# Reordering the hand-over from a linear recurrent layer to attention: convolutions, logits and GELUs issued at other places

## The chip, the cores and the metric

The kernel runs on one core of a Trainium2 chip. A core has five engines that matter here: TensorE (PE: matrix products and transposes), VectorE (DVE), ScalarE (ACT: activations), GpSimd (POOL) and SyncE (SP, which here only issues DMAs). Each engine works through its own list of instructions in order and waits on semaphores for the others. The metric is the device time of one execution in microseconds (us); the median of several runs is compared.

## The reference, cut to what matters

One transformer-like block on x of shape (4, 1024, 256) in float32:

```python
x = x + lru(layernorm(x))     # linear recurrence over time, then an MLP with exact GELU and a layer norm
x = x + ffn(layernorm(x))     # the "first FFN"
x = x + attention(layernorm(x))   # 8 heads of 64, keys and values from a rank-64 latent
x = x + ffn(layernorm(x))     # the "last FFN", same weights
```

The FFN is the unusual part. For each token it forms two score vectors of 256 (`so` and `si`):

```python
xc = einsum('ngf,gf->ng', x.reshape(n, 64, 4), conv_w) + conv_b    # a grouped "convolution": 256 -> 64
xn = (xc - mean_over_tokens) * rsqrt(var_over_tokens + eps) * gamma + beta
score = softmax(gelu(xn) @ lin_w.T + lin_b)
top 32 of 256 scores are kept, all others are zero
out = (x @ W) * top32(score_so) + (x * top32(score_si)) @ W + bias
```

The mean and the variance go over all 4096 tokens. So no GELU of an FFN can start before the last token has passed through the layer before it and its convolution.

## The kernel before

**Tiles.** The 4096 tokens are 32 tiles of 128 tokens (128 partitions, 256 features). Four tiles are a block; there are 8 blocks (NBLK), two for each of the four batch rows. x stays on chip in float32 for the whole kernel, and every sublayer updates it in place.

**Order of the work.** The program is Python that issues instructions through generators. A generator (`head`, `tile`, `outputs`, `ahead`, `prepare`) yields at stage borders, and the loops in `tile_kernel` advance several of them by turns with `next`. A scheduler of the framework then orders the instructions of each engine by a simulated timeline; `with tc.issue_after(ins)` keeps what is issued inside it behind the named instruction. So the diff moves calls, and what it does to an engine's order has to be read from the built program.

**The LRU's end (lines 1105 to 1116).** `outputs` (L422) makes the LRU's output for a block: products into `po`, bias to `ot` (L438), a product into `pz` and GELU to `zt` (L446), a second product `pz2` (added to `ot` on VectorE, L455), transposes to `py` (L465), layer norm (statistics on VectorE, applied on ScalarE as `yn`, L474), and the update of x (L479, L480). For the last block, number 7, this is done in two halves of 256 tokens, and line 1110 fixes how their steps alternate. `f1.head(blk)` (L501) is the first FFN's start for a block: layer norm statistics of the updated x, normalised tiles `xn` (ScalarE, L145), transposes to `pt` (TensorE, L147), a copy `ft` (ScalarE, L524), which also goes to DRAM as `tt` through SP's queue (L527), the convolution `pc` (TensorE, L529), its bias to `xc` (ScalarE, L533), and statistics of `xc` (VectorE, L534). A head has two pairs of tiles, each with its own `xn`, `pt`, `ft`. Heads 0 to 4 are issued earlier; head 5 behind the last GELU of the LRU, head 6 behind the last `yn`, head 7 in two halves at the end.

**The first FFN's first eight tiles (lines 1126 to 1168).** `norm_scale` (L538) turns the statistics into `bs` and `bt`. `gelu(blk)` (L585, instruction at L587) applies GELU to one block of `xc` in place, on ScalarE. GELU and Exp are in different activation tables; `warm` (L151) issues one tiny activation so that the table is loaded at a chosen place. `tile(i)` (L589) does one tile: logits into `pl` (TensorE, L554 and L556), the largest 8 (VectorE, L674), `nm` (GpSimd, L613), exponentials `ex` and `e` (ScalarE, L615 and L618); then three more rounds of max and match_replace on VectorE (L674) and the difference `ex` (L628); then the output branch `pf` (TensorE, L567) scaled to `ob` (ScalarE, L650); then the input branch `xg` (ScalarE L657, times `ex` at L658), transposed to `px` (L682), copied to `vt` (ScalarE, L697), multiplied into `pf` (L699) and added to x (VectorE, L662). `ahead(blk)` (L571) computes the products `pfa` of later blocks (L567), copies them to `pfs` (ScalarE, L581) and stores them (L582). `pf` and `pfa` share two PSUM buffers, `px` has one, `pl` two (line 1129). Only blocks 0 and 1 are tiled here; the other 24 tiles are worked off inside attention, so the GELUs of blocks 2 to 7 are not read before that. `attn_weights` prepares the attention weights beside it, and `prepare`, `latents`, `values` and `queries` (keyed by the loop index in `places`, line 1148) start attention's first batch row: layer norm, `xn`, `pt`, `xnt`, latent product `pml` (L170), `kh` and `kl`. Attention proper begins with the first score product `sc` (L881).

**The rest.** Attention (`heads`, L856) runs with a list of side jobs placed by `merge` (L952), and the last FFN (from line 1198) runs 32 tiles like the eight above, with one GELU ahead and seven behind the exponentials of an early tile.

Of the kernel before, what the change touches and what calls it, by code (L numbers as in the profile page):

```python
# [26 lines left out]
TPB = T // P  # L27
# [123 lines left out]
def warm(nc, pool, func):  # L151

    t = pool.tile([P, 1], F32, tag="warm", name="warm")
    nc.gpsimd.memset(t, 0.0)
    nc.scalar.activation(t, t, func)
# [818 lines left out]
def run(*gens):  # L974
    for g in gens:
        for _ in g:
            pass
# [51 lines left out]
def tile_kernel(ctx: ExitStack, tc: tile.TileContext, x_in, w_lru, vecs_in, rows, w_ffn, lin_t, w_attn, w_down, out):  # L1029
# [34 lines left out]
    with ExitStack() as c1:  # L1064
        psum = Banks(c1.enter_context(tc.tile_pool(name="ps1", space=PSUM)), {"pu": 2, "po": 2, "py": 2, "pt": 2})

        brow = c1.enter_context(tc.tile_pool(name="brow", bufs=1)).tile([P, 2, D], F32, tag="brow", name="brow")
        lru = Lru(tc, c1, ident, vecs, brow, w_lru, psum)
        xb = [x[4 * k : 4 * k + 4] for k in range(NBLK)]
        xnt = [lru.head(xb[0])]  # L1070
        lru.tables(lambda: xnt.append(lru.head(xb[1])))
        with tc.issue_after(lru.xnt_first):
            for blk in range(2, 4):
                load_x(nc.scalar, blk)
        h = [[lru.states(xnt, c) for c in range(KD)]]
        lru.output_weights()
        with tc.issue_after(lru.evacuated[3]):
            nc.scalar.dma_start(brow.rearrange("p a b -> p (a b)"), rows[0, 2 * D : 4 * D].partition_broadcast(P))
        xnt += [lru.head(xb[k]) for k in (2, 3)]
        h.append([lru.states(xnt[2:4], c) for c in range(KD)])  # L1080
        for k in range(NBLK):
            last = k >= NBLK - 2
            if k == 0:
                with tc.issue_after(lru.evacuated[7]):
                    for blk in range(4, NBLK):
                        load_x(nc.scalar, blk)
                    ffn_weights(
                        nc, c1.enter_context(tc.tile_pool(name="rows", bufs=1)), cp, w, lint, lin_t, w_ffn, rows
                    )
            if k < NBLK - 1:  # L1090
                run(lru.outputs(k % CH, xb[k], xnt[k], h[k // CH], (0, 1), last))

            b = k // CH + 1
            if 2 <= b < B:
                if k % CH == 0:
                    h.append([])
                h[b].append(lru.states(xnt[b * CH : (b + 1) * CH], k % CH))
            if k + 4 < NBLK:
                xnt.append(lru.head(xb[k + 4]))
            if 2 <= k < NBLK - 2:  # L1100
                run(f1.head(k - 2, lru.sp, psum, "pt"))
        for blk in range(4, NBLK - 3):
            run(f1.head(blk, lru.sp, psum, "pt"))
        k = NBLK - 1
        ot, zt = lru.buffers()
        halves = [
            lru.outputs(k % CH, xb[k], xnt[k], h[k // CH], (i,), last, tag, [v[:, :, c : c + 256] for v in (ot, zt)])
            for i, tag, c in ((0, "pu", 0), (1, "po", 256))
        ]
        for i in (0, 0, 1, 0, 1, 0, 1, 0, 1, 1):  # L1110
            next(halves[i])
        with tc.issue_after(lru.last_gelu):
            run(f1.head(NBLK - 3, lru.sp, psum, "pt"))
        with tc.issue_after(lru.last_yn):
            run(f1.head(NBLK - 2, lru.sp, psum, "pt"))
        run(*(f1.head(NBLK - 1, lru.sp, psum, "pu", (i,), "lx", "zt") for i in range(2)))

    with ExitStack() as c2:
        sp = c2.enter_context(tc.tile_pool(name="at_s", bufs=2))
        wp = c2.enter_context(tc.tile_pool(name="at_w", bufs=1))  # L1120
        two = lambda shape, name: [wp.tile(shape, F32R, tag=f"{name}{i}", name=f"{name}{i}") for i in range(2)]
        wqk, wvo, wd = two([P, KD, HEADS * HD], "wqk"), two([P, PAIRS, D], "wvo"), two([P, KD, P], "wd")
        wfs = two([P, KD, D], "wf")
        nc.scalar.copy(wfs[0], w.wf)
        nc.gpsimd.tensor_tensor(wfs[1], w.wf, wfs[0].bitcast(F32), ALU.subtract)
        at = Attention(tc, x, ident, ident64, wqk, wvo, wd, sp, wp)
        with ExitStack() as c4:
            psum = Banks(
                c4.enter_context(tc.tile_pool(name="ps4", space=PSUM)), {"pl": 2, "px": 1, "pf": 2, "at": 3}
            )  # L1130
            fp = c4.enter_context(tc.tile_pool(name="f_t", bufs=4))
            weights = attn_weights(nc, fp, psum, "at", w_attn, w_down, wqk, wvo, wd, at, ident64)
            f1.norm_scale(sp)
            tts = [f1.load(blk, fp, f"tt{blk}") for blk in range(2)]
            f1.gelu(0)
            with tc.issue_after(f1.gelu(1)):
                for blk in range(2, NBLK):
                    g = f1.gelu(blk)
            with tc.issue_after(g):
                warm(nc, sp, AF.Exp)  # L1140
            tiles = [
                f1.tile(i, fp, psum, ("pl", "px", "pf"), fast=i == TPB - 1, tt=tts[i // 4]) for i in range(TPB)
            ]
            aheads = chain(*(f1.ahead(blk, fp, psum, "pf") for blk in range(2, NBLK)))
            first = at.prepare(0, 0, psum, "at")
            second = at.prepare(0, 1, psum, "at", ((0, 1), (2,), (3,)), False)
            queries = at.queries(0, 0, 0, psum, "at")
            places = {4: [first] * 2, 5: [first] * 2 + [at.values(0, 0, psum, "at")], 7: [queries] + [second] * 4}
            f1.keep = True
            next(tiles[0])  # L1150
            logits = f1.last_logits
            for i in range(TPB + 1):
                if i + 1 < TPB:
                    next(tiles[i + 1])
                if i < TPB:
                    next(tiles[i])
                    next(tiles[i])
                    with tc.issue_after(logits):
                        next(weights, None)
                if i:  # L1160
                    run(tiles[i - 1])
                for steps in places.get(i, []):
                    next(steps)
                for _ in range(2 if i else 0):
                    next(aheads, None)
            run(second)
            f1.keep, f1.last_topk = False, None
        psum = Banks(c2.enter_context(tc.tile_pool(name="ps2", space=PSUM)), {"sc": 2, "t": 2, "s": 2})
        at.hp = c2.enter_context(tc.tile_pool(name="at_h", bufs=1))
        fp = c2.enter_context(tc.tile_pool(name="f_s", bufs=2))  # L1170
        side = []
        for b in range(B):
            n = STEPS * b
            side += [
                (n + nb * 32 + 8 * g - 7, at.queries(b, nb, g, psum, "s"), 1)
                for nb in range(2)
                for g in range(PAIRS)
                if b or nb or g
            ]
            side.append((n + 33, at.output(b, 0, psum), 1.5))  # L1180
            side.append((n + STEPS - 1 if b == B - 1 else n + STEPS + 1.5, at.output(b, 1, psum, range(2 if b == B - 1 else 4)), 1 if b == B - 1 else 1.5))
            side.append((n + 40 if b == B - 1 else n + STEPS + 24, f2.head(2 * b, sp, psum, "s"), 2))
            last = b == B - 1
            side.append((n + STEPS if last else n + STEPS + 8, f2.head(2 * b + 1, sp, psum, "s", (0,) if last else (0, 1)), 1 if last else 2))
            if b < B - 1:
                side.append((n + 38, chain(at.prepare(b + 1, 0, psum, "s"), at.values(b + 1, 0, psum, "s")), 1.5))
                side.append((n + 56, chain(at.prepare(b + 1, 1, psum, "s"), at.values(b + 1, 1, psum, "s")), 1.5))
        side.append((1, at.values(0, 1, psum, "s"), 1))
        for i in range(TPB, NT):
            n = i - TPB  # L1190
            start = 1 + 6.75 * n if n < TPB else STEPS * (n // TPB) - STEPS + 48.25 + 8 * (n % TPB + 1)
            side.append((start, f1.tile(i, fp, psum, "sss", parts=wfs, fine=True), [1, 1, 1, 1, 1, 2, 1]))
        merge(chain(*(at.heads(b, psum) for b in range(B))), side)
        run(at.output(B - 1, 1, psum, range(2, 4)), f2.head(NBLK - 1, sp, psum, "s", (1,)))
# [107 lines left out]
```

## Time and profile before

| what | us |
|---|---|
| median of 3 runs (1536.07 to 1539.59) | 1538.0 |
| the profiled execution's own time | 1533.81 |
| span of its instructions | 1532.1 |
| busy: PE / DVE / ACT / POOL | 1297.4 / 1182.9 / 1014.5 / 681.6 |
| last convolution output `xc` of the first FFN starts (L533) | 291.55 |
| first GELU starts (L587) | 296.48 |
| first exponential starts (L615) | 303.94 |
| first score product of attention starts (L881) | 378.31 |
| first GELU of the last FFN starts (L587) | 1330.91 |

All times within the execution are from the span's start. The span is what the profile shows from first to last instruction; the execution's own time is 1.7 us longer, and both belong to one execution, which is 4.2 us shorter than the median of the runs. A line of a timeline names start, duration, engine, source line, operation, output and input with their shapes and a count, and in brackets how long the engine was idle before it and what released it. Consecutive instructions of one kind are merged.

### The profile page before, as it was taken

Reading aid. Unit: us, or ns where it says so; the run is one execution under the profiler, and the core shown is the slowest. Engines: PE = TensorE matmul, PEld = TensorE weight load, DVE = VectorE, ACT = ScalarE, POOL = GpSimd, SP = SyncE. Lnnn points to the kernel's source line nnn. Section 1 sums busy time; section 2 is a strip of 40 time slices with the busy share of each in tenths; the row PEclk is TensorE's granted clock in tenths of the full one; section 3 lists DMA queues with packets and bytes.
Section 4 is the critical chain, followed back from the end, with each engine's and each line's share of the span. In section 5 each row is a group of like instructions: output and inputs, shape, how many; then the busy total and the mean of one; then the engine's idle time right before and its main releaser. Section 6 shows DMA issues by size and latency. Waiting matters only on the chain. (4 is left out here: it accounts for less than half of the span.)

```text
span 1532.1 us, 28693 instructions
## 1 busy us (share of the span) xinstructions
PE 1297.4 (85%) x10136; PEld 960.2 (63%) x10136; DVE 1182.9 (77%) x3674; ACT 1014.5 (66%) x2145; POOL 681.6 (44%) x848
## 2 busy tenths in 40 slices
PE   4879998698898898898998889888999998657786
PEld 3635455365676766766776767677777776334554
DVE  8976665697878887878778687777676675499998
ACT  5353433664787777787777787877777776476664
POOL 2033333162545454544543554454443534157776
PEclk9999999698999999999999999999999999789888
DMA  3010000331454334344433345434444454000000
GB/s 117 32 41 15 21 21 14 135 101 44 76 91 90 70 70 80 67 80 77 85 76 60 65 85 81 66 60 85 78 75 88 83 95 83 1 11 24 25 25 28
DMA packets 288609, 96.51 MB, mean 63 GB/s; under 512 B 268233, under 2 KB 284626, under 8 KB 288466
## 3 DMA queue, kind: packets, MB, share of 16 engines
q1 hardware_dynamic: 283024, 88.50, 29.0%
q10 hardware_dynamic: 5442, 6.18, 1.2%
q8 instruction: 80, 1.31, 0.3%
q14 instruction: 63, 0.52, 0.1%
HBM read 16.01 MB, written 11.53 MB: 18 GB/s over the span
## 5 line engine op out<-in xcount | busy, mean ns | idle before, releaser
L893 POOL TENSOR_TENSOR pd<-pr,pd 128x1024 f16<-128x1024 f32 x128 | 273.5, 2142 | 256.5 <-ACT pd L892 198.6
L885 DVE TENSOR_REDUCE nm<-sc 128x1 f32<-128x1024 f32 x256 | 308.5, 1218 | 76.8 <-PE sc L881 75.3
L889 ACT ACTIVATE pr<-sc,nm 128x1024 f32<-128x1024 f32 x256 | 285.9, 1120 | 89.8 <-DVE nm L887 53.3
L881 PE MATMUL sc<-kh,qs 128*128 128x512 f32 x512 | 184.9, 439 | 27.1 <-ACT pr L889 19.5
L881 PE MATMUL sc<-kl,qs 128*128 128x512 f32 x512 | 162.4, 398 | 0.0
L674 DVE MATCH_REPLACE8 wk<-m,wk 128x256 f32<-128x256 f32 x384 | 158.3, 419 | 0.1
L905 ACT COPY p<-ptp 128x512 f32<-128x512 f32 x224 | 124.3, 590 | 46.3 <-PE ptp L900 38.2
L900 PE MATMUL ptp<-ident,pr 128*128 128x128 f32 x1024 | 140.2, 277 | 15.6 <-ACT pr L889 14.8
L674 DVE MAX8 m<-wk 128x8 f32<-128x256 f32 x384 | 153.0, 424 | 0.4
L925 PE MATMUL pmo<-p,la 128*64 128x128 f32 x2048 | 142.3, 287 | 5.6 <-ACT ft L524 2.9
L900 PEld LDWEIGHTS ptp<-ident,pr 128*128 128x128 f32 x1024 | 117.1, 141 | 38.0 <-ACT pr L889 24.9
L892 ACT CAST pd<-pr 128x1024 f16<-128x1024 f32 x128 | 133.3, 1055 | 5.9 <-DMA d<-pd 4.8
L925 PEld LDWEIGHTS pmo<-p,la 128*64 128x64 f32 x2048 | 121.5, 143 | 24.2 <-ACT ft L524 5.1
L881 PEld LDWEIGHTS sc<-kh,qs 128*128 128x128 f32 x512 | 85.6, 196 | 51.9 <-ACT pr L889 30.8
L881 PEld LDWEIGHTS sc<-kl,qs 128*128 128x128 f32 x512 | 97.1, 190 | 23.4 <-issue 1.4
L925 PE MATMUL pmo<-d,lb 128*64 128x128 f16 x3072 | 101.8, 221 | 7.6 <-DVE qs L853 2.5
L925 PEld LDWEIGHTS <-lb 128*64 128x64 f16 x3072 | 91.2, 111 | 25.4 <-issue 19.5
L628 POOL TENSOR_TENSOR ex<-ex,wk 128x512 f32<-128x512 f32 x61 | 77.6, 1273 | 50.8 <-DVE wk L674 41.7
L921 POOL COPY rows<-rs 128x128 f32<-128x128 f32 x128 | 36.2, 295 | 125.5 <-PE pmo L933 69.3
L936 DVE TENSOR_TENSOR on<-pmo,rb 128x128 f32<-128x128 f32 x128 | 36.5, 285 | 66.8 <-ACT rb L935 66.2
L699 PE MATMUL pf<-wf,vt 128*128 128x256 f32 x288 | 84.4, 438 | 3.6 <-ACT vt L697 3.6
L147 PE MATMUL pt<-ident,xn 128*128 128x128 f32 x256 | 48.2, 308 | 42.5 <-ACT xn L145 30.6
(306 smaller groups left out, 2789.0 us busy)
## 6 DMA issues: line engine op xcount, KB each, us to landing
tt<-ft SPq DMA_DIRECT2D x16, 256.0 KB
tt<-tt SPq DMA_DIRECT2D x8, 512.0 KB
out<-x SPq DMA_DIRECT2D x32, 128.0 KB
x<-in_x ACTq DMA_DIRECT2D x6, 512.0 KB
pf<-pfs SPq DMA_DIRECT2D x12, 256.0 KB
full<-pf SPq DMA_DIRECT2D x24, 128.0 KB
d<-pd SPq DMA_TRANSPOSE x128
wa<-in_w_attn SPq DMA_DIRECT2D x2, 640.0 KB
```

The costliest lines, as they stand in the source:

```text
L147: nc.tensor.transpose(pt[:, k, i * P : (i + 1) * P], xn[:, k * P : (k + 1) * P], ident)
L628: pool.tensor_tensor(ex, ex, wk, ALU.subtract)
L674: ins = make(*args).ins
L699: nc.tensor.matmul(dst, vt[:, k, :], w.wf[:, k, :], start=(k == 0 and bias is None), stop=(k == KD - 1))
L881: nc.tensor.matmul(sc[:, sl], qs[:, j, q * P : (q + 1) * P], kk[:, sl], start=(i == 0), stop=(i == 1))
L885: nc.vector.tensor_reduce(nm, sc, AX.X, ALU.max, negate=True)
L889: nc.scalar.activation(pr, sc, AF.Exp, bias=nm, accum_out=ssum[:, j : j + 1])
L892: nc.scalar.copy(pd[:, 0, :], pr)
L893: nc.gpsimd.tensor_tensor(pd[:, 1, :], pr, pd[:, 0, :], ALU.subtract)
L900: nc.tensor.transpose(pt[:, kk, :], pr[:, kc * P : (kc + 1) * P], self.ident)
L905: nc.scalar.copy(dst, pt)
L925: nc.tensor.matmul(po[j * HD : (j + 1) * HD, 0, :], v, pts[j][:, c, :], start=(n == 0), stop=(n == len(terms) - 1),)
```

## The change

Three edits in `tile_kernel`. First, head 5 of the first FFN is issued after three steps of block 7's halves, with no condition, and head 6 behind the LRU's last GELU; before, these were the last GELU and the last `yn`. Second, the third step of a tile (difference, `pf` and `ob`) is moved inside the `with` that puts it behind the first tile's logits. Third, the GELUs of blocks 2 to 7 are issued behind the exponentials of tile 7, and with them a second `warm(Exp)`; the first `warm(Exp)` comes behind the GELU of block 1.

```diff
-        for i in (0, 0, 1, 0, 1, 0, 1, 0, 1, 1):
+        for i in (0, 0, 1):
+            next(halves[i])
+        run(f1.head(NBLK - 3, lru.sp, psum, "pt"))
+        for i in (0, 1, 0, 1, 0, 1, 1):
             next(halves[i])
         with tc.issue_after(lru.last_gelu):
-            run(f1.head(NBLK - 3, lru.sp, psum, "pt"))
-        with tc.issue_after(lru.last_yn):
             run(f1.head(NBLK - 2, lru.sp, psum, "pt"))
         run(*(f1.head(NBLK - 1, lru.sp, psum, "pu", (i,), "lx", "zt") for i in range(2)))
...
             f1.gelu(0)
             with tc.issue_after(f1.gelu(1)):
-                for blk in range(2, NBLK):
-                    g = f1.gelu(blk)
-            with tc.issue_after(g):
                 warm(nc, sp, AF.Exp)
...
                 if i + 1 < TPB:
                     next(tiles[i + 1])
+                if i + 2 == TPB:
+
+                    with tc.issue_after(f1.last_exp):
+                        for blk in range(2, NBLK):
+                            g = f1.gelu(blk)
+                    with tc.issue_after(g):
+                        warm(nc, sp, AF.Exp)
                 if i < TPB:
                     next(tiles[i])
-                    next(tiles[i])
                     with tc.issue_after(logits):
+                        next(tiles[i])
                         next(weights, None)
```

## The prediction

> **What bounds the kernel now.** I read the page's table of 40 slices, then a table of busy time by stage, then ScalarE's timeline, then the chain of waits at the end. In the slices:
>
> ```profile
> PE   4879998698898898898998889888999998657786
> DVE  8976665697878887878778687777676675499998
> ACT  5353433664787777787777787877777776476664
> PEclk9999999698999999999999999999999999789888
> ```
>
> A slice is 38.3 us. Slice 8 (268 to 306 us) is where the LRU hands over to the first FFN: TensorE drops to 6 tenths, its clock to 6. The change acts only from 250 to 378 us; the 920 us of attention and the last FFN keep their instructions. By stage:
>
> ```profile
> core 0: us, PE busy (x) PEld busy (x) DVE busy (x) ACT busy (x) POOL busy (x), PEclk, DMA share, GB/s
> 250.00:272.00 22.00, 22.00 (x116) 17.69 (x114) 12.62 (x54) 7.63 (x16) 5.52 (x8) 1.00 0.04 12
> 272.00:292.10 20.10, 11.46 (x49) 5.15 (x50) 12.66 (x84) 12.48 (x24) 0.10 (x1) 0.64 0.22 76
> 296.50:305.10 8.60, 7.38 (x24) 5.09 (x25) 2.24 (x10) 8.57 (x17) 1.68 (x4) 0.72 0.82 311
> 305.10:359.00 53.90, 51.62 (x235) 37.08 (x235) 53.00 (x235) 32.73 (x92) 31.13 (x45) 0.94 0.28 98
> 359.00:378.30 19.30, 13.98 (x57) 10.22 (x55) 12.59 (x49) 7.79 (x17) 1.79 (x3) 0.78 0.04 14
> ```
>
> TensorE is full until 272 (22.00 of 22.00), then nothing is: a latency chain through all four engines, at a clock of 0.64. From 296.5 ScalarE is full (8.57 of 8.60) while VectorE does 2.24 us. From 305.1 to 359 VectorE is full (53.00 of 53.90): the top-32 of eight tiles. The last 19 us are again a chain. ScalarE's timeline in the two holes:
>
> ```profile
> 276.15 1.01 ACT L474 ACTIVATE yn<-py,ly_rs 128x256 f32<-128x256 f32 x2
> 278.28 1.02 ACT L474 ACTIVATE yn<-py,ly_rs 128x256 f32<-128x256 f32 x2 [1.12 <-DVE ly_rs L136]
> 279.19 1.09 ACT L145 ACTIVATE xn<-x,norm_f 128x256 f32<-128x256 f32 x2
> 284.44 1.09 ACT L145 ACTIVATE xn<-x,norm_f 128x256 f32<-128x256 f32 x2
> 291.55 0.47 ACT L533 ACTIVATE xc_f<-pc,vecs 128x256 f32<-128x256 f32 x1 [1.22 <-PE pc L529]
> 296.48 5.75 ACT L587 ACTIVATE xc_f<-xc_f,bt,bs 128x512 f32<-128x512 f32 x8 [2.98 <-DVE bt L548]
> 302.24 1.28 ACT L155 ACT_TABLE_LOAD   x1
> 303.94 0.47 ACT L615 ACTIVATE ex<-pl,nm 128x256 f32<-128x256 f32 x1
> ```
>
> Block 7's LayerNorm applies at 276.15 and 278.28; then head 6 (from 279.19) and head 7 (from 284.44) follow until the last convolution output at 291.55. All statistics wait for that, so GELU starts at 296.48; eight of them and a table load hold the first exponential until 303.94. The last FFN, in the chain that ended last, has the shape that the change gives the first:
>
> ```profile
> 1330.91 0.82 ACT xc_f L587
> 1331.78 2.09 PE pl L556 x2
> 1333.89 0.78 DVE m L674 x2
> 1334.97 0.56 ACT ex L615 x2
> ```
>
> From one GELU to the first exponential it takes 4.06 us; here it is 7.46 (303.94 - 296.48).
>
> **What the Trainium skill says.** "ScalarE: Activation LUTs", section "What ACT_TABLE_LOAD costs": a switch is 1283 ns of load plus some 1380 of drain. The trace agrees on the load (1.28), but the next ScalarE instruction is there 0.01 us later, so I take 1.3. "TensorE: Matmul & The Clock Gate", "What's actually happening": after an idle window of about 3.4 us the array runs at half speed, until as long a busy one. The trace agrees: after 4.33 us idle four transposes take 1.18 us (279.84), before it 0.60 (271.34). Same page, "Architectural detail: the array is 16× 32×32, not 1× 128×128": ScalarE and VectorE are strict FIFOs. So the order of the built program, which I compared on each engine, fixes who queues behind whom.
>
> **Step A, convolutions move up.** Nothing is added or removed. Head 5 (two groups of four transposes, two of four convolution records) moves from between 271.3 and 275.5 to between 261.9 and 270, where TensorE is full. By start-to-start times a group of transposes takes 0.53 us (271.34 to 271.87), one of pc 0.58 (272.95 to 273.53): 2 x 0.53 + 2 x 0.58 = 2.2 us ahead of block 7's second half, less one 0.53 that stood ahead of its last transposes anyway, plus 0.4 for GELUs behind head 5's copies on ScalarE: py ends at 275.0, not 272.95. The hole from 272 on has one head's work less. Head 6 no longer waits for the last yn (279.3): its xn come from about 277.3, when its norm is done, ahead of block 7's yn in ScalarE's order. Queued behind them: two yn at 278.5 (were 276.15), then xn, ft, xn of head 6 (0.5 + 0.6 + 0.6), then the last two yn at 281.1 (was 278.28), and behind these VectorE's x update, block 7's statistics and norm at about 286.6 (was 283.3), xn, and the same 5.1 us from xn to the last xc: 293.2 for 291.55. That is 1.7 us later. Bounds: if yn came in time, head 7 would start with its norm at 283.4, not 284.44, and its two pairs would not sit behind head 6's transposes: 1.75 earlier. If all 2.7 us of the x update's delay stays: 2.7 later. I take 1.0 later, since the walk charges every cold TensorE group in full. SP's queue moves with it: head 5's two tt stores go earlier, and nothing waits.
>
> **Step B, logits ahead.** The pf matmuls of tiles 0 and 1 (eight records, 3.75 us from 296.87) stood ahead of the first logits (300.41). After: first GELU done at 297.3, logits 2.09 us cold: MAX8 at 299.45 for 301.96. pf comes behind; its readers (ob) are not due until 306.
>
> **Step C, six GELUs move.** ScalarE at the start: two GELUs to 298.0, load to 299.3, first exponential at 296.48 + 4.06 = 300.54, 3.4 us earlier. VectorE also takes tile 1's MAX8 first (its logits, half cold, at 301.2), so MATCH_REPLACE starts at 302.1 for 305.10: 3.0 earlier. Six small operations on the weights' norm (0.15 us each, L731 to L738), until now in VectorE's idle time, land in its full stretch: +0.5. Net 2.5 us, and VectorE stays full to the end of tile 7's top-32.
>
> At the end ScalarE gets, behind tile 7's exponentials (about 344.0, in the times of before): load 1.28, five GELUs 3.7, an ob 0.45, one GELU 0.7, load 1.28, warm 0.2 = 7.6 us. From 346.8 to 356.0 ScalarE did 3.35 us of work in before, so the block fits by sum; but what is queued behind it are vt, xg, pfs, pfs, ob, until 351.6. The two pf buffers are a ring through ScalarE and VectorE: TensorE's next side product waits for that ob (349.4), idle from 343.8. From there TensorE alone has 13.7 us to tile 7's last product: pfa 4 x 1.73, pf 2 x 0.9, px 2 x 0.22, pt 2 x 0.55, sums 3 x 1.14. With a wait of 0.3 for pfs it ends at 363.4, and the x update of tile 7 at 363.6 for 365.05; kh at 365.0 for 366.80: a gain of 1.7. But 5.6 us idle is more than the window of the clock, so the first pfa probably takes 3.46: the gain is then about 0.3. Bounds: 2.5 gained (the block hidden); 2.6 lost (half speed for three products, rival 2). I take 1.5 gained, nearer to the warm case, because the window floats and single matmuls may fall in the gap.
>
> **Sum.** Own time 1533.8 (span 1532.1 and 1.7 around it): + 1.0 - 1.5 = 1533.3. The median of the runs shown is 1538.0, 4.2 above; on it: 1537.5. Attention (about the same order) and the last FFN (VectorE full, the same instructions in other order) I cost at nothing, +-1.
>
> **Rivals.**
> 1. Faster: yn gets through and TensorE stays warm. -1.75 - 2.5 = -4.25: 1533.7. For it: ScalarE does 12.48 us in 20.1 at A's place and 3.35 in 9.2 at C's. Against: FIFO order, yn behind xn.
> 2. Slower: the ring behind the GELU block. TensorE idles from 343.8 to 349.4, and at half speed two pfa and one pf cost 2 x 1.73 + 0.87 = 4.3 more: 4.3 - 1.7 = 2.6 lost, and A's 1.0: 1541.6. For it: a clock of 0.64 to 0.78 in every hole. It decides from 4 us of half-speed excess. Against: before also waits there for a buffer (1.41 us at 353.5) without cooling.
> 3. Nothing: VectorE's gain of 2.5 us meets the same tail, A costs nothing: 1538.
>
> **How the numbers follow.** 0.2% is 3.1 us, about what a measurement of this kernel can tell from no change. Forecast 1537.5 with rival 3: 0.42, own range 1535 to 1541. Rival 1 and partial forms of it: 0.37. Rival 2: 0.21. Faster 0.37, same 0.42, slower 0.21; range 1532 (rival 1 with 1.7 for the attention's phase) to 1542.5 (rival 2 with 1).
>
> **What would show it.** A: last xc_f of L533 later than 291.55, yn of block 7 behind head 6's xn; earlier refutes it. B: first MAX8 within 3 us of the first GELU. C: first exponential 4.1 us behind it; two table loads and six GELUs from about 344; pfa behind them at 0.43 us a matmul or double; the x update of tile 7 (365.05) and the first sc (378.31) less than 3 us earlier, counted from bt. I am wrong if the first sc moves by more than 3 us, or if attention's length changes.

## The result and the profile after

The changed kernel takes 1532.2 us in the median of 8 runs, the kernel before 1536.9 in 8 runs beside it: ratio 0.9963, 95% interval 0.9951 to 0.9974. A second measurement with 12 runs gave 0.9967 (0.9953 to 0.9981). So it is some 5 us faster, where 0.5 us was forecast. The time lies inside the range that was given, just above its lower end, but the likeliest case (nothing to be seen) did not come.

The two profiled executions hide this: 1533.81 us before, 1534.08 after. The slices of the page after:

```profile
PE   5879998697898898888988989899999998666775
...
DVE  8976665697878887878778687776676675499998
ACT  5353433466887877797778687877776776476664
...
PEclk9989999699999999999999999999999999679888
```

They differ from those of before in single digits. The reason that the spans agree is ahead of the change: the order of instructions is the same up to block 7's first output row (the first of the four L438 that write its `ot`), yet this row comes at 253.45 us before and at 255.18 after. Over all 20 executions profiled in this study it came between 251.70 and 256.03. So every time below is counted from that row, and the four traces of each kernel are averaged:

| us after block 7's first output row | before | after | difference | on record |
|---|---|---|---|---|
| last convolution output `xc` (L533) | 38.11 | 39.13 | +1.02 | +1.0 |
| first MAX8 (L674) | 48.43 | 47.03 | -1.4 | -1.5 |
| first exponential (L615) | 50.49 | 48.11 | -2.4 | -2.4 |
| first MATCH_REPLACE (L674) | 51.90 | 49.20 | -2.7 | -2.0 |
| last MATCH_REPLACE of tile 7 | 105.30 | 101.83 | -3.5 | -1.5 |
| last x update of the eight tiles (L662) | 111.86 | 110.00 | -1.9 | -0.5 |
| first score product (L881) | 125.19 | 122.42 | -2.8 | -0.5 |
| 33rd score product with `kh` (L881) | 179.37 | 175.88 | -3.5 | -0.5 |

(The column on record is A's +1.0 put together with the prediction's times for B and C.) From the 33rd score product to the last FFN's first GELU it is 899.8 us in both (898.0 to 902.9 in single traces). From there to the end it is 202.4 before (201.2 to 204.0) and 201.1 after (200.7 to 201.4). The sum, 3.5 + 0.0 + 1.4 = 4.9 us, is about what the timed runs show. It is an average of four traces each: attention alone scatters by 4.9 us between traces of one kernel, so a microsecond there could not be seen.

ScalarE's timeline of the changed kernel, at the two places that the prediction showed of before:

```profile
278.76 1.09 ACT L145 ACTIVATE xn<-x,norm_f 128x256 f32<-128x256 f32 x2 [4.83 <-DVE ly_t L65]
279.76 1.00 ACT L474 ACTIVATE yn<-py,ly_rs 128x256 f32<-128x256 f32 x2
...
294.31 0.47 ACT L533 ACTIVATE xc_f<-pc,vecs 128x256 f32<-128x256 f32 x1 [1.22 <-PE pc L529]
...
299.24 1.52 ACT L587 ACTIVATE xc_f<-xc_f,bt,bs 128x512 f32<-128x512 f32 x2 [2.99 <-DVE bt L548]
...
303.30 0.47 ACT L615 ACTIVATE ex<-pl,nm 128x256 f32<-128x256 f32 x1 [1.04 <-POOL nm L613]
```

Head 6's first two `xn` (278.76) now stand ahead of block 7's `yn` (279.76, and a second pair at 282.12). From the first GELU to the first exponential it takes 4.06 us (303.30 - 299.24), as forecast; it was 7.46. The stretches of the changed kernel, by the same events as the prediction's table:

```profile
core 0: us, PE busy (x) PEld busy (x) DVE busy (x) ACT busy (x) POOL busy (x), PEclk, DMA share, GB/s
...
278.76:299.24 20.48, 9.95 (x34) 3.97 (x34) 13.33 (x65) 10.46 (x21) 1.50 (x4) 0.51 0.27 94
299.24:304.30 5.06, 4.20 (x9) 2.31 (x10) 1.50 (x5) 4.00 (x8) 0.19 (x1) 0.62 0.96 323
304.30:357.70 53.40, 47.48 (x220) 35.60 (x219) 51.87 (x231) 36.77 (x96) 31.69 (x47) 0.94 0.32 109
357.70:377.92 20.22, 17.02 (x87) 13.51 (x85) 14.32 (x56) 10.87 (x24) 2.78 (x5) 0.92 0.11 40
```

VectorE does 51.87 us of work in the 53.40 of the top-32 stretch: still nearly full. In the last stretch TensorE now works 17.02 of 20.22 us at a clock of 0.92; it was 13.98 of 19.30 at 0.78. The GELU block at the end, on ScalarE, and the side products beside it, on TensorE:

```profile
348.00 3.63 ACT L587 ACTIVATE xc_f<-xc_f,bt,bs 128x512 f32<-128x512 f32 x5
351.54 0.45 ACT L650 ACTIVATE ob<-pf,rs 128x256 f32<-128x256 f32 x1
...
352.71 1.28 ACT L155 ACT_TABLE_LOAD   x1
354.00 0.20 ACT L155 ACTIVATE warm<-warm 128x1 f32<-128x1 f32 x1
```

```profile
348.01 1.99 PE L567 MATMUL pfa<-wf,tt 128*128 128x256 f32 x8 [1.58 <-DVE x L662]
352.05 1.99 PE L567 MATMUL pfa<-wf,tt 128*128 128x256 f32 x8 [2.04 <-ACT ob L650]
355.49 1.13 PE L567 MATMUL pf<-wf,tt 128*128 128x256 f32 x4 [1.45 <-ACT pfs L581]
```

The block is there as forecast: a table load from 346.70 (1.28, not shown), five GELUs 3.63, an `ob` 0.45, one GELU 0.80 (not shown), a load 1.28 and the tiny activation 0.20. But TensorE's wait is not one piece of 5.6 us: it is 1.58, 2.04 and 1.45 us with a product in each pause, and eight `pfa` records take 1.99 us at 348.01 and at 352.05, which is full speed (before, eight such records took 1.89 or 1.99 us). In the chain that ended last, the last FFN starts as before, with the GELU and the logits; only here the chain lists four records of logits behind it, 3.79 us, where before it listed two (2.09): the last FFN is in another order too:

```profile
1331.70 0.82 ACT xc_f L587
1332.57 3.79 PE pl L556 x4
```

### The profile page after: what moved, and what is told of

It is laid out like the page before. It is cut to its first block, busy times and chain, and to the rows that moved or that the text cites. A ratio compares the mean times of both kernels' runs of the same rounds, so it can differ in the third digit from the quotient of the medians.

```text
span 1532.4 us, 28699 instructions
## 1 busy us (share of the span) xinstructions
PE 1295.5 (85%) x10136; PEld 960.3 (63%) x10136; DVE 1183.2 (77%) x3674; ACT 1017.3 (66%) x2148; POOL 681.6 (44%) x849
## 5 line engine op out<-in xcount | busy, mean ns | idle before, releaser
L881 PE MATMUL sc<-kh,qs 128*128 128x512 f32 x512 | 185.4, 440 | 26.3 <-ACT pr L889 18.7
L881 PE MATMUL sc<-kl,qs 128*128 128x512 f32 x512 | 163.2, 399 | 0.0
L674 DVE MATCH_REPLACE8 wk<-m,wk 128x256 f32<-128x256 f32 x384 | 154.8, 406 | 0.1
L674 DVE MAX8 m<-wk 128x8 f32<-128x256 f32 x384 | 150.2, 412 | 0.4
L881 PEld LDWEIGHTS sc<-kh,qs 128*128 128x128 f32 x512 | 85.8, 196 | 50.9 <-ACT pr L889 29.9
L881 PEld LDWEIGHTS sc<-kl,qs 128*128 128x128 f32 x512 | 97.7, 191 | 23.5 <-issue 1.4
```

What stands on the lines that cost most here:

```text
L674: ins = make(*args).ins
L881: nc.tensor.matmul(sc[:, sl], qs[:, j, q * P : (q + 1) * P], kk[:, sl], start=(i == 0), stop=(i == 1))
```

## Experiments

Every version with a ratio was timed against the kernel before; the others are single runs with a trace. Stage times of a version are those of its one trace, unless more are named. "First row" is block 7's first output row. The recorded expectations name stretches in the same way.

### Controls: both kernels again

No edit.

> The unchanged kernel, as a control with span and clock of every run. Stage theory (the change shifts the first FFN by about 2.6 us, and the rest of the difference of the medians is chance in the clock): ratio 1.000, spans around 1534 us, and mean granted clock about 0.941, the same as in the runs of the changed kernel (mean 0.9425), so that equal clocks leave 2 to 3 us between the two. Clock theory (the change itself spares half-clock windows): mean clock 0.937 or lower here, and at equal clock less than 1 us between the two kernels.

Ratio 0.9999 (0.9986 to 1.0012), 1536.75 us. The first half of the clock theory came true: the mean granted clock is 0.937 in these 14 runs and 0.942 in the 20 runs of the changed kernel. The second half did not: a straight line of time over clock, fitted with one slope to 186 runs of the kernel before (these 14 among them) and the 20 of the changed one, leaves 2.6 us between the two at equal clock. By this estimate about half of the difference of the means (5.4 us) goes with the clock. Some of that is made in the changed stage: TensorE's half-speed time from 250 to 400 us is 47.8 us in all four traces before, and 44.4, 37.5, 37.5 and 37.5 us after. How much of the rest is chance stays open.

> The changed kernel again, as a control beside the other versions, with span and clock of every run. If the first measurement holds: ratio 0.9963 (0.995 to 0.9975), mean granted clock 0.9425 against 0.936 of the kernel before, about 2 us of difference at equal clock and the rest through the clock. If it was chance: ratio 0.998 to 0.999, what the stage's 2.6 us give, and a clock within 0.002 of that of before.

Ratio 0.9967 (0.9953 to 0.9981). The gain is real. The expectation for chance, 0.998 to 0.999, lies outside the interval of the first measurement (up to 0.9974) and touches this one only at its edge.

> The unchanged kernel once more, for a third trace of it: from block 7's first output row to the 33rd first-half score product 179.3 us (179.1 and 179.5 so far), from there to the last FFN's first GELU 898 to 903, from there to the end 201.2 to 202.4. If the gain of the changed kernel beyond the stage is in attention, this middle stretch is longer than the 900.0 and 898.2 of the changed kernel by 2 us; if not, it scatters around 900 in both.

> The changed kernel once more, for a third trace of it: 176.5 and 175.2 us so far for the first stretch (3.4 less than before), 900.0 and 898.2 for attention, 200.7 and 201.4 for the last FFN. Stage theory: 175 to 177 again, and the other two stretches within the scatter of before. If the last FFN's other order of instructions gives 0.7 us, it is 201.5 or less here.

First stretch 179.7 and 175.7, attention 900.0 and 898.1, last FFN 202.1 and 201.4.

> The unchanged kernel, fourth trace: 179.4 us for the first stretch (179.1 to 179.7 so far). If attention gives the rest of the gain: 900 to 903 us for it, longer than in the changed kernel (898.3 to 902.9 so far); if chance, anywhere from 898 to 904.

> The changed kernel, fourth trace: 175.8 us for the first stretch (175.2 to 176.5 so far). If attention gives the rest of the gain: 898 to 900 us again for it (898.1 to 900.0 so far); if chance, anywhere from 898 to 904.

First stretch 179.2 and 176.1; attention 898.0 before and 902.9 after, the reverse of what would be needed if attention gave part of the gain. With these the averages of attention agree to 0.01 us: no gain of attention is to be seen. The last FFN is 204.0 before and 200.8 after.

### Step A alone

```diff
-        for i in (0, 0, 1, 0, 1, 0, 1, 0, 1, 1):
+        for i in (0, 0, 1):
+            next(halves[i])
+        run(f1.head(NBLK - 3, lru.sp, psum, "pt"))
+        for i in (0, 1, 0, 1, 0, 1, 1):
             next(halves[i])
         with tc.issue_after(lru.last_gelu):
-            run(f1.head(NBLK - 3, lru.sp, psum, "pt"))
-        with tc.issue_after(lru.last_yn):
             run(f1.head(NBLK - 2, lru.sp, psum, "pt"))
```

> Step A alone: head 5 after three steps of block 7's halves, head 6 behind the last GELU; logits and GELUs as before. On record: the last convolution output 1.0 us later (bounds 1.75 earlier, 2.7 later), measured from block 7's first output row, ratio about 1.0005. Rival (block 7's norm gets through, the hole shrinks): 1.75 us earlier, ratio 0.999. Stage theory, read from the changed kernel's trace against that row: 1.0 later at the first GELU and at the first score product.

Ratio 1.0033 (1.0011 to 1.0056): slower, by more than any theory gave, with single runs from 1533.5 to 1556 us. The last `xc` is 39.14 us after the first row, the recorded +1.0. The 33rd score product is at 185.1 us, 5.7 late, in its one trace, and more than half of that is lost in the first tiles (columns as above; five us each):

```profile
310.00:315.00 5.00, 5.00 (x14) 2.06 (x14) 5.00 (x21) 3.10 (x6) 4.34 (x5) 0.50 0.00 0
315.00:320.00 5.00, 5.00 (x16) 2.67 (x15) 2.46 (x12) 1.97 (x7) 2.94 (x5) 0.50 0.01 3
```

TensorE is busy without a pause at a clock of 0.50, and VectorE, which should be full, has work for 2.46 of 5 us: at half speed TensorE is the bound of these tiles in this trace. Before, the clock was 0.50 from 310 to 315 and 1.00 from 315 on, with VectorE at 5.00 and 4.71.

### The halves of step A

Head 5 alone (head 6 stays behind the last `yn`):

```diff
-        with tc.issue_after(lru.last_gelu):
+        with tc.issue_after(lru.last_yn):
             run(f1.head(NBLK - 2, lru.sp, psum, "pt"))
```

(on top of step A's diff)

> Half of step A: head 5 moves up, head 6 stays behind the last yn, the rest as before. On record: head 5's groups delay block 7's second half by about 2 us, head 6 behind yn as before, so the last convolution output comes 1 to 2 us later than before (38.1 us after block 7's first output row). If head 6 ahead of yn is what costs, it comes within 0.3 us of before. If the 0.33% that step A lost alone is due to the longer hole without TensorE work (and so to the clock), the half-clock time from 250 to 400 us is 55 us or more here too; if it was chance, 38 to 48 us as in the other versions and ratio 1.000.

```profile
281.48 1.02 ACT L474 ACTIVATE yn<-py,ly_rs 128x256 f32<-128x256 f32 x2 [2.18 <-DVE fx_mv L134]
...
294.76 0.47 ACT L533 ACTIVATE xc_f<-pc,vecs 128x256 f32<-128x256 f32 x1 [1.22 <-PE pc L529]
```

The last `xc` is 40.20 us after the first row: +2.1. Block 7's last `yn` waits until 281.48 (26.9 after the first row; 24.8 before). Ratio 1.0021 (1.0011 to 1.0032), though the 33rd score product is 0.8 us early. Two further traces:

> Head 5 alone, second trace. If attention is entered in a worse state: 902 to 906 us from the 33rd score product to the last FFN's first GELU, as in its first trace (904.3), with three or more half-clock windows more than the changed kernel there. If that was chance: 898 to 903, the range of the traces of the kernels before and after.

> Head 5 alone, third trace: as in the second, 902 to 906 us of attention if the entry decides, 898 to 903 if it is chance.

Last `xc` +2.1 in both; attention 904.2 and 906.1 after 904.3 in the first trace: 5 us longer than in both kernels, every time, while the first stretch was 178.6 to 178.9. Before these two traces, head 5 alone was taken to have the changed kernel's order of instructions in attention. The traces say otherwise: 74 lines of difference in 8424 TensorE records. The edit has re-planned attention. That this order is what makes it longer is likely, not shown: the version with the filled hole, below, has the changed kernel's order on TensorE there, and took 904.8 us in its one trace.

Head 6 alone, which stands ahead of `yn`:

```diff
-        with tc.issue_after(lru.last_yn):
+        with tc.issue_after(lru.last_gelu):
             run(f1.head(NBLK - 2, lru.sp, psum, "pt"))
```

> Head 6's half of step A alone, one trace. Last convolution output 37.0 us after block 7's first output row if its move gives 1.1 us by itself, 38.1 if it only repairs what head 5's move spoils, 38.5 or later if its xn ahead of yn cost as in the walk on record.

```profile
278.07 1.09 ACT L145 ACTIVATE xn<-x,norm_f 128x256 f32<-128x256 f32 x2
279.30 1.02 ACT L474 ACTIVATE yn<-py,ly_rs 128x256 f32<-128x256 f32 x2
```

The last `xc` is 36.67 us after the first row: 1.4 earlier, against the walk on record. The first pair of `yn` starts 22.70 us after the first row, as in the kernel before (276.15 - 253.45), and head 6's two `xn` fill a pause of ScalarE between the pairs. This trace had 175.3 us to the 33rd score product, in one run of 1530.9 us. From that product to the end, PE, DVE, ACT and POOL work through the changed kernel's order record by record, the re-planned last FFN included, and the last FFN takes 201.4 us here. So this one line brings, in its only run, the lead at the 33rd score product and the new last FFN without B, C or head 5. Whether it is as fast as the whole change is the rival that these experiments leave open: it was not timed over several runs.

> B and C with head 6 behind the last GELU, head 5 where it was before. If head 6's move gives 1.1 us wherever head 5 stands, the last convolution output starts 37.0 us after block 7's first output row (38.1 before, 39.1 in the changed kernel), the 33rd score product at 173.8 us (175.9 in the changed kernel), and the time is about 2 us under the changed kernel's, ratio 0.995, unless attention or the last FFN come out in another order and take that back. On record (head 6's xn ahead of block 7's yn delay what follows): 38.5 us or later, 33rd score product at 176 us or later, ratio 0.9965 or more.

Last `xc` 36.66, first MATCH_REPLACE 47.0 (changed kernel 49.2), but the 33rd score product at 176.1, as in the changed kernel. 2.2 us of lead at the start of the top-32 are gone at its tail. Ratio 0.9994 (0.9982 to 1.0005): it does not beat the changed kernel.

### Steps B and C

B and C without A:

> Steps B and C without A. On record: 1.5 us gained, ratio 0.999. Stage theory: 3.6 us gained at the first score product measured from block 7's first output row (2.6 of the whole change plus the 1.0 that A costs), so ratio 0.9975 by the stage alone, and this version is about 1 us faster than the whole change, 0.996 where the whole change has 0.9963 with 2.5 us that the stage does not explain. If A is what gains, this one is slower than the whole change: 0.998 or more.

The 33rd score product is at 175.6 us, the changed kernel's 175.9. So B and C reach this lead without A, and the 1.0 us that A costs at the last `xc` is not paid at the stretch's end. They reach it on another way, with a top-32 of 55.2 us (52.6 in the changed kernel), and as head 6 alone reaches it too, the lead can't be split among the steps. The last FFN is 202.5 us, the old length. Ratio 0.9989 (0.9976 to 1.0002): the whole change, at 0.9967, is rather the faster, though the intervals overlap at their ends.

B alone:

```diff
                     next(tiles[i])
-                    next(tiles[i])
                     with tc.issue_after(logits):
+                        next(tiles[i])
                         next(weights, None)
```

> Step B alone: the third step of a tile behind the first tile's logits; convolutions and GELUs as before, so all eight GELUs and the table load still stand ahead of the first exponential. On record: the first MAX8 2.5 us earlier, but the first exponential not (303.9 in the times of before), so no time gained: ratio 1.000. If B alone gives what B and C together give at the first match_replace (3.3 us earlier from block 7's first output row), C is worth nothing: ratio 0.998.

First MAX8 46.0 (2.4 earlier), first MATCH_REPLACE 51.0 (0.9 earlier, not 3.3): as on record. But ratio 1.0037 (1.0025 to 1.0049). Its one trace puts the loss in attention: 908.5 us, 9 more than in both kernels, with 434 lines of difference to before in 8424 TensorE records.

C alone:

```diff
             with tc.issue_after(f1.gelu(1)):
-                for blk in range(2, NBLK):
-                    g = f1.gelu(blk)
-            with tc.issue_after(g):
                 warm(nc, sp, AF.Exp)
...
+                if i + 2 == TPB:
+                    with tc.issue_after(f1.last_exp):
+                        for blk in range(2, NBLK):
+                            g = f1.gelu(blk)
+                    with tc.issue_after(g):
+                        warm(nc, sp, AF.Exp)
```

> Step C alone: six GELUs and a second table load behind tile 7's exponentials, the side product pf still ahead of the first logits. On record the first exponential is 3.4 us earlier only with B as well; the first MAX8 stays at 301.96 - 253.45 = 48.5 us after block 7's first output row, so the first match_replace starts about 1.5 us after it, 1.6 us earlier than before; ratio 0.999. If B is worth nothing the first match_replace is as early as with B and C together (2.6 us earlier). Rival (the GELU block at the end holds the ring of side products and eats what the start gains): tile 7's update of x no earlier than before, ratio 1.000 or more.

Ratio 0.9998 (0.9985 to 1.0010): the rival holds. The last MATCH_REPLACE of tile 7 starts 1.6 us early, the x update 2.6 us late. ScalarE and TensorE at the block:

```profile
345.89 4.34 ACT L587 ACTIVATE xc_f<-xc_f,bt,bs 128x512 f32<-128x512 f32 x6
```

```profile
352.25 2.08 PE L567 MATMUL pf<-wf,tt 128*128 128x256 f32 x4 [5.81 <-ACT pfs L581]
```

No `ob` stands between the six GELUs here. TensorE waits 5.81 us in one piece, and four `pf` records then take 2.08 us, twice the 1.03 that they take at full speed (at 344.10 in the changed kernel). This is the mechanism of rival 2 of the prediction; its loss of time did not come, as the 33rd score product is only 0.4 us late. The order of attention and of the last FFN in this version is that of before.

### The ring and the place of the block

```diff
-                c4.enter_context(tc.tile_pool(name="ps4", space=PSUM)), {"pl": 2, "px": 1, "pf": 2, "at": 3}
+                c4.enter_context(tc.tile_pool(name="ps4", space=PSUM)), {"pl": 2, "px": 1, "pf": 3, "at": 2}
```

> The changed kernel with three PSUM buffers for the side products pf and pfa in place of two (and two in place of three for the attention weights and prepare). Ring theory (step C and rival 2 on record: TensorE's next side product waits for the ob that is queued behind the GELU block): the idle time of TensorE beside the block (5.1 us in three gaps in the first trace of the changed kernel) halves, and from the end of tile 7's top-32 to its update of x it takes 6.5 us in place of 8.2; ratio 0.9957. Rival (TensorE has more work than room there anyway, or the missing third bank of the attention weights costs as much): 8 us or more, ratio 0.9967 to 0.9975.

```profile
353.94 3.73 PE L567 MATMUL pfa<-wf,tt 128*128 128x256 f32 x8 [6.39 <-ACT pfs L581]
```

Ratio 1.0031 (1.0022 to 1.0041). The tail, from tile 7's last MATCH_REPLACE to its x update, is 8.6 us (8.2 in the changed kernel): the ring theory's remedy fails. With three buffers the planner puts no `ob` between the GELUs, so that the six come in one piece; TensorE waits 6.39 us for a `pfs` behind them and runs the next eight records at half speed, 3.73 us. Yet the x update is only 0.4 us later than in the changed kernel. The loss comes behind it: 15.0 us from the x update to the first score product (12.4). The missing bank for `prepare` is the likely reason; it was not tested alone.

```diff
-                if i + 2 == TPB:
+                if i + 3 == TPB:
```

> The changed kernel with the six GELUs behind tile 6's exponentials in place of tile 7's. Tile 7's exponentials were there 5.6 us ahead of the match_replace that needs them (90.1 and 95.7 us after block 7's first output row), so a block of 7.6 us costs VectorE at most 2 us. Ring theory: the tail from tile 7's top-32 to its update of x goes back from 8.2 to 6.5 us as TensorE has time to catch up; net 0 to 1.7 us gained, ratio 0.9955 to 0.997. If the block's place doesn't matter (ScalarE has room): tail 8.2 us again and ratio 0.997. If VectorE stalls for tile 7's exponentials by more than 2 us: ratio 0.998 or more.

```profile
347.16 3.68 PE L567 MATMUL pfa<-wf,tt 128*128 128x256 f32 x8 [4.14 <-ACT ob L650]
```

Ratio 0.9990 (0.9978 to 1.0002). The tail shrinks to 7.1 us as expected, but TensorE is held for 4.14 us in the middle of the tiles, is at half speed behind it, and VectorE idles 2.4 us in two waits beside it (1.21 for an exponential, 1.19 for a side product): tile 7's top-32 ends 2.5 us later than in the changed kernel.

### The hole filled

```diff
+            with tc.issue_after(f1.convolved):
+                fill = psum.tile([P, 512], "at", "fill")
+                for _ in range(5):
+                    nc.tensor.matmul(fill[:, 0:256], ident, w.wf[:, 0, :], start=True, stop=True)
             f1.norm_scale(sp)
```

(and one such product of 128 columns in each of the last head's two convolutions)

> The changed kernel with TensorE kept busy by products that nobody reads: one in each gap of the last head's two convolutions and five between the last convolution and the first logits. Nothing of the computation is left out. Clock theory: the half-clock windows from 290 to 303 us go, the first logits take 0.9 us in place of 2.1, the first MAX8 is 1 to 1.5 us earlier from block 7's first output row than in the changed kernel (47.0 us), the half-clock time between 250 and 400 us falls from 44 to about 30 us, and the time falls by 2 to 4 us against the changed kernel: ratio 0.994 to 0.9955. Stage theory without the clock: VectorE's top-32 bounds from the first match_replace on, the gain is the 1 us of the logits alone: 0.9955 to 0.996.

```profile
310.00:315.00 5.00, 5.00 (x17) 4.02 (x17) 4.37 (x18) 1.39 (x3) 4.75 (x6) 0.50 0.01 3
```

The clock is 1.00 from 300 to 305 us (not shown; 0.62 from 299.24 to 304.30 in the changed kernel), and the first MATCH_REPLACE 0.9 us earlier. But from 310 to 315 it is 0.50 again with TensorE busy throughout, the half-speed time from 250 to 400 us is 44.4 us as in the first trace of the changed kernel, VectorE waits 2.64 us for an exponential at 317, and the ratio is 0.9985 (0.9970 to 1.0000). The trace belongs to the slowest of 22 runs (1542.3; their median is 1532.9), but the median too shows nothing gained over the changed kernel. Full speed at the logits does not keep the clock, so the clock theory in that form fails. What takes the clock away from a busy TensorE there stays open. In 15 of the 20 traces a half-speed stretch begins 1.5 to 4.2 us after the first of the small 64x64 products of `attn_weights` (L742 of the kernel before); no run moved these products.

## Why the prediction was wrong, step by step

**Step A** was right in its value and wrong in its working, so the agreement is in part luck. The recorded +1.0 us is +1.02 in four traces. The 2.05 us that the walk gave to head 5 is 2.1 in three. But the walk let head 6's `xn` delay block 7's `yn` and then took something off; on the chip head 6 gives 1.1 to 1.4 us back, since its `xn` fall into a pause. "FIFO order, yn behind xn" is no cost where the `xn` fill a pause of ScalarE, as with head 6 alone.

**Step B and the start of step C** were right: MAX8 -1.4 for -1.5, first exponential -2.4 for -2.4.

**The failed steps** are the end of step C, "I take 1.5 gained", and two terms of the sum that were put at nothing: the way from tile 7's x update to attention, and the last FFN. Here they are in order of time, with the length of the top-32 ahead of them.

**"Net 2.5 us, and VectorE stays full to the end of tile 7's top-32".** VectorE did stay full, but the lead there is 3.5 us with A's cost already paid, not 1.5. 0.7 of the missing 2.0 is there at the first MATCH_REPLACE. The rest is in the length of the top-32, 52.6 us for 53.4, where the prediction had added 0.5. The small operations of L731 to L738 did come in (0.4 us of VectorE's time), but the planner took one x update (L662) with its statistics (L133, L134) and parts of the norm chain (L55, L56, L64) out of this stretch, 1.3 us, to behind tile 7's top-32. VectorE's busy time in it is 52.0 us in all four traces, for 52.9 or 53.0 before. VectorE's timeline behind that top-32, first before, then in the changed kernel:

```profile
360.61 0.41 DVE L662 TENSOR_TENSOR x<-x,pf 128x256 f32<-128x256 f32 x1
...
365.05 0.42 DVE L662 TENSOR_TENSOR x<-x,pf 128x256 f32<-128x256 f32 x1 [1.17 <-PE pf L699]
```

```profile
357.92 0.42 DVE L662 TENSOR_TENSOR x<-x,pf 128x256 f32<-128x256 f32 x1
...
364.31 0.42 DVE L662 TENSOR_TENSOR x<-x,pf 128x256 f32<-128x256 f32 x1 [0.55 <-PE pf L699]
...
365.58 0.40 DVE L662 TENSOR_TENSOR x<-x,pf 128x256 f32<-128x256 f32 x1
```

Three updates stand here where before there were two. This work was put off, not saved: from the first MATCH_REPLACE to the last x update the changed kernel takes 60.8 us, the one before 60.0.

**"I take 1.5 gained".** From the last MATCH_REPLACE to the last x update it takes 8.2 us for 6.6, a loss of 1.6 where the prediction's numbers (2.5 gained, 1.5 left) say 1.0. Counted from the last `xc`, so without A's cost, the x update still comes 2.9 us earlier, not 1.5. The prediction was right that TensorE and the ring decide here: behind its third pause (the 1.45 us above) TensorE works without a gap of more than 0.15 us up to tile 7's x update, in all four traces. What it had wrong is the pause itself, "TensorE idles from 343.8 to 349.4": eight records of `pfa` ran inside it (348.01 us), and no product behind it was at half speed. How much the split is worth is not shown. With the pause in one piece the x update, counted from the last `xc`, is only 0.4 us later than in the changed kernel in the ring of three and 1.7 in B and C without A (4.86 us of waiting, then half speed), but 5.5 in C alone.

**What is late next** was not followed to the end. From the x update to the first score product it is 12.4 us for 13.3, and to the 33rd another 0.7 less: 1.6 us together that the prediction had at nothing. In the first trace pair TensorE's clock in the last stretch is 0.92 for 0.78, perhaps because the delayed side products keep it at work there; but one of the four traces after has 13.2 us all the same, so this is argued, not shown.

**"Attention and the last FFN I cost at nothing"** holds for attention (0.0) and not for the last FFN: 1.4 us shorter, with 380 lines of difference in its 810 VectorE records. C alone, with the old order, has 203.1 us, the old length. In the five traces with the old order it is 201.2 to 204.0 us, in the five with the new one (head 6 alone among them) 200.7 to 201.4. That the new order is the cause fits this, but the two ranges touch, and head 5 alone, which has yet another order, is at 201.6 to 202.5; it is not settled.

The sum: 2.0 (to the end of the top-32) - 0.6 (its tail) + 1.6 (to the 33rd score product) + 1.4 (last FFN) = 4.4 us on top of the forecast 0.5. Of the rivals, number 1 gave the nearest time (1533.7) for a half-right reason: TensorE stayed warm, but `yn` did not get through. "I am wrong if the first sc moves by more than 3 us" was met: counted from `bt`, as the prediction counts, it moved by 3.8 us (2.8 from the first row).

Three figures of the working do not come out of the lines, though none is a term of the sum. Where it says "the 920 us of attention and the last FFN", the two are 1154 (378.31 to 1532.1). In step A "all 2.7 us of the x update's delay" is 2.8 by its `yn` (281.1 - 278.28) and 3.3 by its norm (286.6 - 283.3). In step C, 1.7 less the 1.73 of one half-speed product is nothing, not 0.3.

## What to carry to other kernels

When a scheduler orders the program, look beyond the edited place on every engine: it can move work out of the stretch of the engine that bounds it (which is a gain only if the work is not waited for behind it), and a small edit can re-plan a stage hundreds of microseconds later. Logits alone had 9 us more of attention in its trace, and head 6 alone, one line, has the changed kernel's last FFN. So time each half of a change alone, over several runs. Count stage times from a common event just ahead of the change, over several traces. And when a block must stand on an engine that feeds TensorE through a ring, look at whether a consumer of the ring gets through in the middle of it: that decides whether TensorE waits in pieces or in one.

## What the runs showed of the hardware

- TensorE's half-speed stretches in the traces' clock record last 3.41 us or whole multiples of it, in every trace of this study (but for a stretch that the end of the program cuts). The time to block 7's first output row, with one and the same order of instructions, varied by 4.3 us between executions; the changed kernel's two profiled extremes there carried 23.9 and 30.7 us of half speed.
- "TensorE: Matmul & The Clock Gate" (section "What's actually happening") of the Trainium skill puts the idle window at about 3.4 us. The runs fit that: behind waits of 1.58 and 2.04 us eight records take 1.99 us, behind 4.14 and 6.39 us they take 3.68 and 3.73. But a TensorE that is busy throughout also ran at half speed (310 to 320 us in step A alone), which the idle window does not explain.
- A table load cost ScalarE its 1.28 us and no more here: in the GELU block the load at 352.71 is followed by the tiny activation at 354.00, 0.01 us after its end, with GELUs directly ahead of it.
